# A message-passing kernel on one core: sums on TensorE's column quarters, and a shorter lead of the gathers

## The chip, the core and the metric

The kernel runs on one core of a Trainium2 chip. The core has five engines with a queue of instructions each: TensorE (PE; its weight loads are listed as PEld), VectorE (DVE), ScalarE (ACT), GpSimd (POOL) and SyncE (SP). They meet through semaphores. TensorE writes PSUM (8 banks of 512 floats a partition), ScalarE and VectorE read and write PSUM and the on-chip memory, DMA moves data between that and DRAM. The metric is the device time of one execution in microseconds (us), the median of the runs shown.

## The reference

12500 nodes with 160 features (64 scalars and 32 vectors of three), 400000 edges sorted by their target `dst`. Cut to what matters:

```
h = relu(layernorm(x))
y0, y1 = h0 @ W_l1_0, h1 @ W_l1_1            # per node, times its attribute
w = silu(edge16 @ fc_W1) @ fc_W2             # per edge: w_a 64, w_b 64, w_c 32, w_d 32
mid_a = w_a * y0[src] * e0                   # 64
mid_d = w_d * sum_c(y1[src] * e1)            # 32
mid_b = (w_b * y0[src])[:, :, None] * e1     # 64 x 3
mid_c = (w_c * e0)[:, :, None] * y1[src]     # 32 x 3
z0[dst] += concat(mid_a, mid_d)              # 96
z1[dst] += concat(mid_b, mid_c)              # 96 x 3
out = x + C_S * (h @ W_sc) + C_X * (z @ W_l2) * attribute
```

Per target node 4 x 96 sums are formed over its edges, z0 and the three components of z1, and go through W_l2_0 (96 x 64) and W_l2_1 (96 x 32).

## The kernel before

**Stages.** A node stage computes layernorm and y for all nodes, writes y to DRAM (`y_d`) and leaves x + C_S * (h @ W_sc) in the on-chip tile `acc`. The edge stage, nearly the whole time, adds the messages into `acc`. A last stage that a flag skips here handles edges that fit no window, and stores the result.

**Tiles of the edge stage.** 128 edges are a tile (3125 of them), 4 tiles a batch `b` (782), 3 tiles a window of at most 32 neighbouring target nodes, 4 windows a group `g` (12 tiles, 3 batches, 261 groups).

**What one batch passes through.**
- `load(b)` (L403): every eighth batch SP reads a block of edge features `xe` (L412); for each tile GpSimd issues one indirect DMA (L417), which gathers the 128 source rows of `y_d` into the batch's buffer `yg`. The pool `yg` has 10 buffers (L388), the lead is AHEAD = 8 batches (L554). In this loop GpSimd does nothing but these gathers.
- `hidden_pair` (L434): two matmuls of 32 rows and 512 columns each (L426) and the silu on ScalarE (L431) serve four batches.
- `weigh(b)` (L440): four matmuls of 64 rows (L448) give the edge weights in PSUM `pw` (2 buffers); ScalarE scales them by e0 (L368, four) and copies e1 and the window row beside them (L369).
- `select(b)` (L472): VectorE builds `sel`, for each edge a row of 32 ones and zeros that marks its node in the window (L479, part 3), and the same times each component of e1 (L481, parts 0 to 2).
- `products(b)` (L484): VectorE multiplies weights and gathered rows into `pr`, 256 columns: mid_a 64, mid_d 32, mid_c 3 x 32, w_b * y0 64 (L374 to L381; L381 is the last).
- `sums(b)` (L491): for each tile one product with `sel` (128 edges x 128 columns, four parts of 32) as weights and all 256 columns of `pr` as the moving side (L499). It accumulates over a window's three tiles in a PSUM bank `pz` (2 buffers). Of the 128 x 256 result only the blocks that belong together are used: part 3 with the first 192 columns, parts 0 to 2 with the last 64. After a window ScalarE copies these four blocks to `zs` (L504 once, L506 three times), so that `zs` has a node in each row and 384 columns.
- For the group before: `turn` (three transposes of `zs`, L514, copied by L516), `linear` (three products with `wo`, L523, copied to `os` by L525; VectorE builds `place`, L527), `add` (L535, moves the rows to their places in two node tiles) and `accumulate` (L544, VectorE adds them into `acc`).

fp32 products take two weight loads and two matmuls each in the trace, transposes one: L499 is 3125 products and 6250 matmuls.

**What sets the order.** The order on TensorE, ScalarE and VectorE is written out by hand (L556 to L595): in iteration b come load(b+8), weigh(b+2), one of turn, linear or add of group g-1, select(b+1), products(b+1), at the last batch of a group accumulate(g-1), then sums(b), and hidden_pair in every fourth. Buffers and semaphores do the rest: a gather waits until its `yg` buffer has been read by the products (L381) of the batch that used it ten batches before.

Of the kernel before, what the change touches and what calls it, by code (L numbers as in the profile page):

```python
# [10 lines left out]
F32 = mybir.dt.float32  # L11
I32 = mybir.dt.int32
AF = mybir.ActivationFunctionType
ALU = mybir.AluOpType
# [4 lines left out]
P = 128  # L19
M0 = 64  # L20
M1 = 32
# [4 lines left out]
PC = 256  # L26
ZC = 384
GT = 4
BT = 32
WN = 32  # L30
WT = 3
GW = 4
TG = WT * GW
EG = 8
GN = 8
HN = 2
LO = D - P
EPS = 1e-5
C_S = math.sin(math.pi / 8.0)
# [4 lines left out]
def kernel(  # L44
# [19 lines left out]
    nc = tc.nc  # L64
# [3 lines left out]
    T = n_edges // P  # L68
# [3 lines left out]
    NB = (T + GT - 1) // GT  # L72
# [9 lines left out]
    const = ctx.enter_context(tc.tile_pool(name="const", bufs=1))  # L82
# [5 lines left out]
    ident = const.tile([P, P], F32, name="ident")  # L88
# [90 lines left out]
    w1 = const.tile([P, 2 * FC_H], F32, name="w1")  # L179
    w2 = const.tile([P, NW], F32, name="w2")  # L180

    wo = const.tile([P, 3, D], F32, name="wo")
    wnr = ip.tile([P, 2, 3 * M1], F32, name="wnr")
    wor = ip.tile([P, 3, D], F32, name="wor")
# [16 lines left out]
    def edge_weight_loads():  # L201
        nc.gpsimd.memset(w1, 0.0)
        for i in range(P // FC_IN):
            nc.sync.dma_start(w1[FC_IN * i:FC_IN * (i + 1), FC_H * (i % 2):FC_H * (i % 2 + 1)], fc_w1)
        for i in range(2):
            for to, of, m in ((0, 0, M0), (M0, 2 * M0, M1), (M0 + M1, M0, M0), (2 * M0 + M1, 2 * M0 + M1, M1)):
                nc.sync.dma_start(w2[FC_H * i:FC_H * (i + 1), to:to + m], fc_w2[:, of:of + m])
        nc.gpsimd.memset(wor, 0.0)

        def o1(c):  # L210
            return slice(M0 + M1 * c, M0 + M1 * (c + 1))

        nc.sync.dma_start(wor[0:M0 + M1, 0, 0:M0], w_l2_0)
        for rows, k, c in ((slice(96, P), 0, 0), (slice(0, 32), 1, 1), (slice(32, 64), 1, 2)):
            nc.sync.dma_start(wor[rows, k, o1(c)], w_l2_1[M0:, :])
        for rows, k, c in ((slice(64, P), 1, 0), (slice(0, 64), 2, 1), (slice(64, P), 2, 2)):
            nc.sync.dma_start(wor[rows, k, o1(c)], w_l2_1[0:M0, :])

    def edge_weights():
        nc.vector.tensor_scalar(w2, w2, 1.0 / math.sqrt(FC_H), None, ALU.mult)  # L220
        f = C_X / math.sqrt(10.0 * (M0 + M1))
        nc.vector.tensor_scalar(wo[:, :, 0:M0], wor[:, :, 0:M0], f, None, ALU.mult)
        nc.vector.tensor_scalar(wo[M0:M0 + M1, 0, 0:M0], wo[M0:M0 + M1, 0, 0:M0], 1.0 / math.sqrt(3.0), None, ALU.mult)
        nc.vector.tensor_scalar(wo[:, :, M0:].rearrange("p k (u c) -> p k c u", c=3),
                                wor[:, :, M0:].rearrange("p k (c u) -> p k c u", c=3), f, None, ALU.mult)
# [27 lines left out]
    with (  # L253
# [82 lines left out]
        with tc.manual_schedule(engines=engines):  # L336
# [7 lines left out]
            last = len(steps) - 1  # L344
            for q in range(len(steps) + 4):
                if q <= last and steps[q][2] == 0:
                    g = steps[q][0] + LEAD * GN
# [35 lines left out]
    with (  # L383
# [1 line left out]
        tc.tile_pool(name="prod", bufs=3) as prod,  # L385
        tc.tile_pool(name="ld", bufs=2) as ld,
        tc.tile_pool(name="ev", bufs=2) as evp,
        tc.tile_pool(name="yg", bufs=10) as ygp,  # L388
        tc.tile_pool(name="hid", bufs=4) as hid,
        tc.tile_pool(name="post", bufs=2) as post,  # L390
        tc.tile_pool(name="p_w", bufs=2, space=PSUM) as p_w,
# [3 lines left out]
        blocks, ev4, hids, rows, wts, sels, z_ps, z_sb, zT, o_sb, prs, sums_ps = ({} for _ in range(12))  # L395
# [4 lines left out]
        def windows_of(g):  # L400
            return min(GW, NWIN - g * GW)

        def load(b):  # L403
            blk = b * GT // BT
            if blk not in blocks:

                xe = ld.tile([P, 512], F32, name="xe")
                v = e16[blk * P:(blk + 1) * P, :].rearrange("(s k f) (h c) -> s h f k c", s=4, k=2, h=2)
                for s in range(4):
                    for h in range(2):  # L410
                        lo = 32 * s + FC_IN * h
                        nc.sync.dma_start(xe[lo:lo + FC_IN, :].rearrange("p (k c) -> p k c", k=2), v[s, h])  # L412
                blocks[blk] = xe
            yg = ygp.tile([P, GT, D], F32, name="yg")
            rows[b] = yg
            for k, t in enumerate(tiles_of(b)):
                nc.gpsimd.indirect_dma_start(  # L417
                    out=yg[:, k, :], out_offset=None, in_=y_d,
                    in_offset=bass.IndirectOffsetOnAxis(ap=src_sb[:, t:t + 1], axis=0))
# [69 lines left out]
            prs[b] = pr  # L489

        def sums(b):  # L491
            pr = prs.pop(b)
            for k, t in enumerate(tiles_of(b)):
                g, w = t // TG, t // WT % GW
                if t % WT == 0:
                    z_ps[g, w] = p_z.tile([P, 512], F32, name="pz")
                pz = z_ps[g, w]
                last = t % WT == WT - 1 or t == T - 1
                nc.tensor.matmul(pz[:, 0:PC], sels[g][:, t % TG, :, :], pr[:, k, :], start=t % WT == 0, stop=last)  # L499
                if last:  # L500
                    if w == 0:
                        z_sb[g] = post.tile([P, ZC], F32, name="zs")
                    pz, zs = z_ps.pop((g, w)), z_sb[g][WN * w:WN * (w + 1), :]
                    nc.scalar.activation(zs[:, 0:192], pz[96:P, 0:192], AF.Copy)  # L504
                    for c in range(3):
                        nc.scalar.activation(zs[:, 192 + M0 * c:192 + M0 * (c + 1)],  # L506
                                             pz[WN * c:WN * (c + 1), 192:PC], AF.Copy)

        def turn(g):

            m, zs = WN * windows_of(g), z_sb.pop(g)
            pt = p_x.tile([P, 3, P], F32, name="px")
            for k in range(3):
                nc.tensor.transpose(pt[:, k, :m], zs[:m, P * k:P * (k + 1)], ident[:m, :m])  # L514
            za = post.tile([P, 3, P], F32, name="za")
            nc.scalar.activation(za[:, :, :m], pt[:, :, :m], AF.Copy)  # L516
            zT[g] = za

        def linear(g):
            m, za = WN * windows_of(g), zT.pop(g)  # L520
            po = p_x.tile([P, D], F32, name="px")
            for k in range(3):
                nc.tensor.matmul(po[:m, :], za[:, k, :m], wo[:, k, :], start=k == 0, stop=k == 2)  # L523
            os = post.tile([P, D], F32, name="os")
            nc.scalar.activation(os[:m, :], po[:m, :], AF.Copy)  # L525
            place = post.tile([P, 2, P], F32, name="place")
            nc.vector.tensor_scalar(place.rearrange("p h n -> p (h n)"), iota, at[:, g:g + 1], None, ALU.is_equal)  # L527
            o_sb[g] = os, place
# [23 lines left out]


        AHEAD = 8  # L554
        K = TG // GT
        order = tc.manual_schedule(engines={mybir.EngineType.PE, mybir.EngineType.Activation, mybir.EngineType.DVE})  # L556
        with order:
            for b in range(min(AHEAD, NB)):
                load(b)
            e4_load(0)  # L560
            e4_join(0)
            hidden_pair(0)
            weigh(0)
            if NB > 1:
                weigh(1)
            select(0)
            products(0)
            for b in range(NB):
                g, k = divmod(b, K)
                if b + AHEAD < NB:  # L570
                    load(b + AHEAD)
                q, r = divmod(b, EG * K)
                if r == 0:
                    e4_load(q + 1)
                if r == EG * K - 4:
                    e4_join(q + 1)
                if b + 2 < NB:
                    weigh(b + 2)
                if g:
                    (turn, linear, add)[k](g - 1)  # L580
                if b + 1 < NB:
                    select(b + 1)
                    products(b + 1)
                if g and k == K - 1:
                    accumulate(g - 1)
                    leave_before(g)
                sums(b)
                if b % 4 == 0 and b + 4 < NB:
                    hidden_pair((b + 4) // 2)
            for h in ([NG - 2] if NG > 1 else []) + [NG - 1]:  # L590
                for k, stage in enumerate((turn, linear, add, accumulate)):
                    if h == NG - 1 or min(k, K - 1) > (NB - 1) % K:
                        stage(h)
                        if k == 3:
                            leave_before(h + 1)  # L595
# [4 lines left out]
    with (  # L600
# [10 lines left out]
        n = nc.values_load(far_i[0:1, 0:1], min_val=0, max_val=1)  # L611
        with tc.For_i(0, n, 1) as _:
            with tc.For_i(0, ZR, P) as r:
                nc.sync.dma_start(z_d[ds(r, P), :], zero)
            with tc.For_i(0, TP // GT, 1) as g:
# [15 lines left out]
                yg = fp.tile([P, GT, D], F32, name="f_yg")  # L631
# [9 lines left out]
                for k in range(GT):  # L641
                    nc.tensor.matmul(pw[:, k, 0:NW], hT[:, P * k:P * (k + 1)], w2[0:FC_H, :],
                                     start=True, stop=True)
                tmp = fp.tile([P, GT, 4, M1], F32, name="f_tmp")
                scale(pw, ev, GT)
                pr = fp.tile([P, GT, PC], F32, name="f_pr")
                multiply(pr, tmp, pw, yg, GT)
                for k in range(GT):
                    pd = fpp.tile([P, P], F32, name="f_pd")
                    nc.tensor.transpose(pd, df[:, k:k + 1].to_broadcast([P, P]), ident)  # L650
                    sel = fp.tile([P, P], F32, name="f_sel")
# [82 lines left out]
```

## Time and profile before

| | us |
|---|---|
| three runs | 5686.64, 5694.77, 5710.15 |
| median | 5694.77 |
| profiled execution | 5716.56 |
| its span | 5714.8 |
| mean granted TensorE clock | 0.776 |

Busy time in the profiled execution: PE 3840.1 us, DVE 2902.1, ACT 2645.1, POOL 3024.8. The matmuls of L499 are busy for 1930.1 us (462 ns each, 6250 of them), the copies of L504 and L506 for 337.8 and 669.8 us, the gathers of L417 for 2983.4 us (955 ns each).

How to read the page: a group's line gives line, engine, operation, what it writes and reads, its count, then after the first bar busy time and mean ns of one, after the second the idle time of the engine just before these instructions and what ended most of it. The chain is followed back from the last instruction; its shares are of the span. A row of the timeline gives start, length, engine, line, operation, count, and in brackets the idle time before and its releaser. "remote" (in the chain: another core or an unknown queue) is what is written where no releaser was found in the semaphore records; "issue" is time in which an engine waited for nothing that the profile shows.

### The profile page before, as it was taken

Reading aid. Unit: us, or ns where it says so; the run is one execution under the profiler, and the core shown is the slowest. Engines: PE = TensorE matmul, PEld = TensorE weight load, DVE = VectorE, ACT = ScalarE, POOL = GpSimd, SP = SyncE. Lnnn points to the kernel's source line nnn. Section 1 sums busy time; section 2 is a strip of 40 time slices with the busy share of each in tenths; the row PEclk is TensorE's granted clock in tenths of the full one; section 3 lists DMA queues with packets and bytes.
Section 4 is the critical chain, followed back from the end, with each engine's and each line's share of the span. In section 5 each row is a group of like instructions: output and inputs, shape, how many; then the busy total and the mean of one; then the engine's idle time right before and its main releaser. Section 6 shows DMA issues by size and latency. Waiting matters only on the chain.

```text
span 5714.8 us, 61466 instructions
## 1 busy us (share of the span) xinstructions
PE 3840.1 (67%) x17265; PEld 2679.8 (47%) x17265; DVE 2902.1 (51%) x7407; ACT 2645.1 (46%) x9217; POOL 3024.8 (53%) x3150
## 2 busy tenths in 40 slices
PE   6476676666666666666667667666667766666766
PEld 5344444444444444444444445444444444444544
DVE  7454455444455455454555445544445554545555
ACT  5244444444444444444444444444444444444445
POOL 3655555555555555555555555555555555555553
PEclk9677777787777777777777777777777778788778
DMA  4211111211111111111112112111111121232211
GB/s 140 62 53 52 53 54 49 54 52 52 52 51 54 52 53 52 52 53 50 54 53 55 51 53 55 52 52 52 51 52 52 54 54 53 54 88 55 55 49 54
DMA packets 233168, 319.85 MB, mean 56 GB/s; under 512 B 65754, under 2 KB 182566, under 8 KB 232566
## 3 DMA queue, kind: packets, MB, share of 16 engines
q0 software_dynamic: 150000, 256.20, 16.7%
q1 hardware_dynamic: 69026, 51.24, 3.1%
q10 hardware_dynamic: 13796, 8.44, 0.5%
q8 instruction: 139, 2.28, 0.2%
q14 instruction: 207, 1.70, 0.1%
HBM read 299.62 MB, written 16.00 MB: 55 GB/s over the span
## 4 chain that ended last, share of the span: by engine, by line
PE 52%; another core or an unknown queue 23%; ACT 13%; issue 8%; DVE 3%; DMA 0%; SPq 0%; DVEq 0%; ACTq 0%
PE pz L499 25%; PE pw L448 10%; PE px L426 6%; ACT pw L368 5%; PE px L514 4%; PE px L523 4%; ACT zs L506 3%; PE px L535 3%; ACT zs L504 2%; ACT pw L369 1%; ACT hT L431 0%; DVE h L283 0%; DVE tmp L376 0%; DVE tmp L374 0%
## 5 line engine op out<-in xcount | busy, mean ns | idle before, releaser
L417 POOL DMA_INDIRECT yg<-y_d,src_sb x3125 | 2983.4, 955 | 2542.2 <-DVE pr L381 1641.0
L499 PE MATMUL pz<-pr,sel 128*128 128x256 f32 x6250 | 1930.1, 462 | 151.1 <-ACT zs L506 114.2
L368 ACT ACTIVATE pw<-pw,ev 128x96 f32<-128x96 f32 x3125 | 985.3, 315 | 1679.1 <-remote 1048.8
L499 PEld LDWEIGHTS pz<-pr,sel 128*128 128x128 f32 x6250 | 1443.4, 242 | 406.4 <-ACT zs L506 132.4
L544 DVE SCALAR_TENSOR_TENSOR acc<-px,a_sb,acc 128x160 f32 x522 | 200.2, 384 | 1765.5 <-remote 1292.0
L514 PE MATMUL px<-ident,zs 128*128 128x128 f32 (+1 forms) x783 | 268.9, 428 | 876.2 <-ACT zs L504 804.3
L448 PE MATMUL pw<-w,hT 64*128 64x192 f32 x6250 | 839.2, 394 | 12.9 <-DVE pr L381 8.1
L448 PEld LDWEIGHTS pw<-w,hT 64*128 64x128 f32 x6250 | 579.6, 216 | 469.4 <-issue 269.8
L426 PE MATMUL px<-xe,w 32*128 32x512 f32 x782 | 415.6, 789 | 526.1 <-remote 422.1
L479 DVE TENSOR_TENSOR sel<-iota,pw 128x128 f32<-128x128 f32 x782 | 223.5, 286 | 951.5 <-ACT pw L369 591.7
L504 ACT ACTIVATE zs<-pz 32x192 f32<-32x192 f32 x1042 | 337.8, 324 | 776.2 <-PE pz L499 312.9
L506 ACT ACTIVATE zs<-pz 32x64 f32<-32x64 f32 x3126 | 669.8, 214 | 41.8
L514 PEld LDWEIGHTS px<-ident,zs 128*128 128x128 f32 (+1 forms) x783 | 130.3, 181 | 1025.9 <-ACT zs L504 857.1
L376 DVE TENSOR_REDUCE tmp<-tmp 128x128 f32<-128x384 f32 x782 | 463.5, 593 | 26.8
L481 DVE TENSOR_TENSOR sel<-sel,pw 128x384 f32<-128x384 f32 x782 | 432.5, 553 | 26.7
L379 DVE TENSOR_TENSOR pr<-pw,yg 128x384 f32<-128x384 f32 x782 | 427.9, 547 | 0.0
L374 DVE TENSOR_TENSOR tmp<-yg,pw 128x384 f32<-128x384 f32 x782 | 427.8, 547 | 0.0
L426 PEld LDWEIGHTS px<-xe,w 32*128 32x128 f32 x782 | 107.8, 227 | 678.2 <-remote 470.9
L535 PE MATMUL px<-os,place 128*128 128x160 f32 x1044 | 236.7, 354 | 207.0 <-issue 175.0
L431 ACT ACTIVATE hT<-px 128x512 f32<-128x512 f32 x391 | 221.6, 596 | 300.5 <-remote 194.0
L377 DVE TENSOR_TENSOR pr<-pw,yg 128x256 f32<-128x256 f32 x782 | 323.6, 414 | 0.0
L378 DVE TENSOR_TENSOR pr<-pw,yg 128x256 f32<-128x256 f32 x782 | 323.4, 414 | 0.0
(83 smaller groups left out, 1902.3 us busy)
## 6 DMA issues: line engine op xcount, KB each, us to landing
yg<-y_d,src_sb POOLq DMA_INDIRECT x3125
xe<-in_e SPq DMA_DIRECT2D x784, 32.0 KB
xt<-in_x SPq DMA_DIRECT2D x12, 640.0 KB
y_d<-ys ACTq DMA_DIRECT2D x12, 640.0 KB
out<-acc SPq DMA_DIRECT2D x11, 640.0 KB
raw<-in_e SPq DMA_DIRECT2D x32, 192.0 KB
dst_i<-in_dst SPq DMA_DIRECT2D x1, 1568.0 KB
src_sb<-in_src SPq DMA_DIRECT2D x1, 1568.0 KB
```

Source lines behind the costliest of these rows:

```text
L368: nc.scalar.activation(pw[:, k, 0:96], pw[:, k, 0:96], AF.Copy, scale=ev[:, k, 0:1])
L374: nc.vector.tensor_tensor(tmp[:, :n, 0:3, :], y1, wt[:, :n, NW:NW + 3].unsqueeze(3).to_broadcast([P, n, 3, M1]), ALU.mult)
L376: nc.vector.tensor_reduce(tmp[:, :n, 3, :], tmp[:, :n, 0:3, :].rearrange("p t c u -> p t u c"), AX.X, ALU.add)
L379: nc.vector.tensor_mul(pr[:, :n, 96:192].rearrange("p t (c u) -> p t c u", c=3), wt[:, :n, M0:96].unsqueeze(2).to_broadcast([P, n, 3, M1]) ...
L417: nc.gpsimd.indirect_dma_start(out=yg[:, k, :], out_offset=None, in_=y_d, in_offset=bass.IndirectOffsetOnAxis(ap=src_sb[:, t:t + 1], axis=0))
L426: nc.tensor.matmul(ph, w1[r, :], xe[r, :], start=True, stop=True)
L448: nc.tensor.matmul(pw[:, k, 0:NW], hT[r, o:o + P], w2[r, :], start=True, stop=True)
L481: nc.vector.tensor_tensor(sel[:, :, 0:3, :], sel[:, :, 3:4, :].to_broadcast([P, n, 3, WN]), wt[:, :n, NW:NW + 3].unsqueeze(3).to_broadcast ...
L499: nc.tensor.matmul(pz[:, 0:PC], sels[g][:, t % TG, :, :], pr[:, k, :], start=t % WT == 0, stop=last)
L504: nc.scalar.activation(zs[:, 0:192], pz[96:P, 0:192], AF.Copy)
L506: nc.scalar.activation(zs[:, 192 + M0 * c:192 + M0 * (c + 1)], pz[WN * c:WN * (c + 1), 192:PC], AF.Copy)
L514: nc.tensor.transpose(pt[:, k, :m], zs[:m, P * k:P * (k + 1)], ident[:m, :m])
```

## The change

**Sums.** `sums` makes seven products for a tile instead of one. The weights are one part of `sel` each, 32 columns wide, and the result goes to 32 of the 128 PSUM partitions, a column quarter of TensorE: parts 0, 1, 2 with w_b * y0 (64 columns) to quarters 0, 1, 2; part 3 with mid_a and mid_d (96 columns) to quarter 3; part 3 again with one component of mid_c (32 columns) to each of quarters 0, 1, 2. A window takes 96 columns of the bank, and all four windows of a group lie side by side in one bank, which is copied once per group, 384 columns of all 128 partitions.

**After the sums.** The quarters now are the four kinds of sums (z1 by component, z0) and the columns the 96 features, so `turn` makes four transposes, one for each window, `linear` four products of 96 rows, one for each kind, against the plain weights `wz` (64 columns for z0, 32 for each component), and `os` is copied in two pieces, the second of which puts the components side by side. `wz` costs two more DMAs and two scalings in the setup; `wo` stays for the last stage.

**Gathers.** `load` is split: `features` keeps the lead of 8 batches, the gathers get RUN = 2 and a pool of 3 buffers instead of 10.

```
+SC = M0 + M1
...
+        nc.sync.dma_start(wz[:, 0:M0], w_l2_0)
+        nc.sync.dma_start(wz[:, M0:], w_l2_1)
...
+        nc.vector.tensor_scalar(wz, wz, f, None, ALU.mult)
+        nc.vector.tensor_scalar(wz[M0:, 0:M0], wz[M0:, 0:M0], 1.0 / math.sqrt(3.0), None, ALU.mult)
...
-        tc.tile_pool(name="yg", bufs=10) as ygp,
+        tc.tile_pool(name="yg", bufs=3) as ygp,
...
-        def load(b):
+        def features(b):
...
+        def load(b):
             yg = ygp.tile([P, GT, D], F32, name="yg")
...
         def sums(b):
             pr = prs.pop(b)
             for k, t in enumerate(tiles_of(b)):
                 g, w = t // TG, t // WT % GW
-                if t % WT == 0:
-                    z_ps[g, w] = p_z.tile([P, 512], F32, name="pz")
-                pz = z_ps[g, w]
-                last = t % WT == WT - 1 or t == T - 1
-                nc.tensor.matmul(pz[:, 0:PC], sels[g][:, t % TG, :, :], pr[:, k, :], start=t % WT == 0, stop=last)
-                if last:
-                    if w == 0:
-                        z_sb[g] = post.tile([P, ZC], F32, name="zs")
-                    pz, zs = z_ps.pop((g, w)), z_sb[g][WN * w:WN * (w + 1), :]
-                    nc.scalar.activation(zs[:, 0:192], pz[96:P, 0:192], AF.Copy)
-                    for c in range(3):
-                        nc.scalar.activation(zs[:, 192 + M0 * c:192 + M0 * (c + 1)],
-                                             pz[WN * c:WN * (c + 1), 192:PC], AF.Copy)
+                if t % TG == 0:
+                    z_ps[g] = p_z.tile([P, 512], F32, name="pz")
+                sel = sels[g][:, t % TG, :, :]
+                first, last = t % WT == 0, t % WT == WT - 1 or t == T - 1
+                for r, part, c, lo, n in [(s, s, 192, 0, M0) for s in range(3)] + [(3, 3, 0, 0, SC)] + \
+                        [(s, 3, SC + M1 * s, M0, M1) for s in range(3)]:
+                    o = SC * w + lo
+                    nc.tensor.matmul(z_ps[g][WN * r:WN * (r + 1), o:o + n], sel[:, part, :], pr[:, k, c:c + n],
+                                     start=first and lo == 0, stop=last and (lo > 0 or r == 3))
+                if t % TG == TG - 1 or t == T - 1:
+                    zs = post.tile([P, GW, SC], F32, name="zs")
+                    n = windows_of(g)
+                    nc.scalar.activation(zs[:, :n, :].rearrange("p w c -> p (w c)"), z_ps.pop(g)[:, 0:SC * n], AF.Copy)
+                    z_sb[g] = zs
...
         def turn(g):
-            for k in range(3):
-                nc.tensor.transpose(pt[:, k, :m], zs[:m, P * k:P * (k + 1)], ident[:m, :m])
-            za = post.tile([P, 3, P], F32, name="za")
-            nc.scalar.activation(za[:, :, :m], pt[:, :, :m], AF.Copy)
+            for w in range(n):
+                nc.tensor.transpose(pt[0:SC, w, :], zs[:, w, :], ident)
+            za = post.tile([SC, 4, GW, WN], F32, name="za")
+            nc.scalar.activation(za.rearrange("p s w n -> p w s n")[:, :n, :, :],
+                                 pt[0:SC, :n, :].rearrange("p w (s n) -> p w s n", n=WN), AF.Copy)
...
         def linear(g):
-            for k in range(3):
-                nc.tensor.matmul(po[:m, :], za[:, k, :m], wo[:, k, :], start=k == 0, stop=k == 2)
+            for r, lo, wd, o in [(3, 0, M0, 0)] + [(s, M0, M1, M0 + M1 * s) for s in range(3)]:
+                nc.tensor.matmul(po[:m, o:o + wd], za[:, r, :n, :], wz[:, lo:lo + wd], start=True, stop=True)
             os = post.tile([P, D], F32, name="os")
-            nc.scalar.activation(os[:m, :], po[:m, :], AF.Copy)
+            nc.scalar.activation(os[:m, 0:M0], po[:m, 0:M0], AF.Copy)
+            nc.scalar.activation(os[:m, M0:].rearrange("p (u c) -> p c u", c=3),
+                                 po[:m, M0:].rearrange("p (c u) -> p c u", c=3), AF.Copy)
...
         AHEAD = 8
+        RUN = 2
...
             for b in range(min(AHEAD, NB)):
+                features(b)
+            for b in range(min(RUN, NB)):
                 load(b)
...
                 if b + AHEAD < NB:
-                    load(b + AHEAD)
+                    features(b + AHEAD)
+                if b + RUN < NB:
+                    load(b + RUN)
```

More of the change, by code (lines that the diff above doesn't have):

```diff
@@ L180 @@
     w2 = const.tile([P, NW], F32, name="w2")
+    wz = const.tile([M0 + M1, M0 + M1], F32, name="wz")
     wo = const.tile([P, 3, D], F32, name="wo")
@@ L509, in turn @@
-        def turn(g):
-            m, zs = WN * windows_of(g), z_sb.pop(g)
-            pt = p_x.tile([P, 3, P], F32, name="px")
-            for k in range(3):
-                nc.tensor.transpose(pt[:, k, :m], zs[:m, P * k:P * (k + 1)], ident[:m, :m])
-            za = post.tile([P, 3, P], F32, name="za")
-            nc.scalar.activation(za[:, :, :m], pt[:, :, :m], AF.Copy)
+                if t % TG == 0:
+                    z_ps[g] = p_z.tile([P, 512], F32, name="pz")
+                sel = sels[g][:, t % TG, :, :]
@@ new lines, in sums @@
+                if t % TG == TG - 1 or t == T - 1:
[3 more added lines that the diff above has]
+                    z_sb[g] = zs
+        def turn(g):
+            n, zs = windows_of(g), z_sb.pop(g)
+            pt = p_x.tile([P, GW, P], F32, name="px")
+            for w in range(n):
[3 more added lines that the diff above has]
+                                 pt[0:SC, :n, :].rearrange("p w (s n) -> p w s n", n=WN), AF.Copy)
@@ L517, in turn @@
             zT[g] = za
         def linear(g):
-            m, za = WN * windows_of(g), zT.pop(g)
+            m, n, za = WN * windows_of(g), windows_of(g), zT.pop(g)
             po = p_x.tile([P, D], F32, name="px")
-            for k in range(3):
-                nc.tensor.matmul(po[:m, :], za[:, k, :m], wo[:, k, :], start=k == 0, stop=k == 2)
+            for r, lo, wd, o in [(3, 0, M0, 0)] + [(s, M0, M1, M0 + M1 * s) for s in range(3)]:
+                nc.tensor.matmul(po[:m, o:o + wd], za[:, r, :n, :], wz[:, lo:lo + wd], start=True, stop=True)
```

## Prediction

> **What bounds the kernel now.** I read the page first: busy shares, chain, costliest groups.
>
> ```profile
> span 5714.8 us, 61466 instructions
> PE 3840.1 (67%) x17265; PEld 2679.8 (47%) x17265; DVE 2902.1 (51%) x7407; ACT 2645.1 (46%) x9217; POOL 3024.8 (53%) x3150
> PE 52%; another core or an unknown queue 23%; ACT 13%; issue 8%; DVE 3%; DMA 0%; SPq 0%; DVEq 0%; ACTq 0%
> L417 POOL DMA_INDIRECT yg<-y_d,src_sb x3125 | 2983.4, 955 | 2542.2 <-DVE pr L381 1641.0
> L499 PE MATMUL pz<-pr,sel 128*128 128x256 f32 x6250 | 1930.1, 462 | 151.1 <-ACT zs L506 114.2
> L448 PE MATMUL pw<-w,hT 64*128 64x192 f32 x6250 | 839.2, 394 | 12.9 <-DVE pr L381 8.1
> L504 ACT ACTIVATE zs<-pz 32x192 f32<-32x192 f32 x1042 | 337.8, 324 | 776.2 <-PE pz L499 312.9
> L506 ACT ACTIVATE zs<-pz 32x64 f32<-32x64 f32 x3126 | 669.8, 214 | 41.8
> ```
>
> The reader is to see that no engine is full, and that 23% of the chain hangs on a releaser which this one-core program should not have. The table of waits says who meets it, the scaling of the weights (L368) and the accumulation (L544), both of which wait for TensorE:
>
> ```profile
> POOL yg L417 <- DVE pr L381: 1641.0, 282, 10.3
> DVE acc L544 <- remote: 1292.0, 166, 9.7
> ACT pw L368 <- remote: 1048.8, 161, 18.7
> ```
>
> The timeline around one such wait:
>
> ```profile
> 3016.54 0.92 PE L448 MATMUL pw<-w,hT 64*128 64x192 f32 x8
> ...
> 3024.34 0.95 POOL L417 DMA_INDIRECT yg<-y_d,src_sb  x1 [0.30 <-issue]
> 3027.44 1.36 ACT L368 ACTIVATE pw<-pw,ev 128x96 f32<-128x96 f32 x4 [7.40 <-remote]
> ...
> 3032.41 0.95 POOL L417 DMA_INDIRECT yg<-y_d,src_sb  x1 [7.12 <-DVE pr L381]
> ```
>
> L448 ended at 3017.46, but ScalarE, which waits for nothing else, could read its result only at 3027.44, 2.2 us after GpSimd's last gather ended (3025.29). Over the whole trace: batches whose L448 ends in the first 5 us of an unbroken run of gathers are seen by ScalarE within a median of 0.04 to 0.24 us; those that end 6 to 9 us into a run, after 8 to 9 us, and nearly always 2.2 us after the run's end. I call this a **hold**: late in a long run of gathers TensorE's completions do not arrive. The trace shows that it happens, not why.
>
> So the loop is a cycle. 196 of the 324 runs have 12 gathers, three batches, 14.8 us (a gather takes 0.95, the next begins 0.30 later). Then GpSimd is idle for 7.2 us: 2.2 until the hold ends, 5.0 for scaling (1.6), selection and products (3.3), whose end frees a buffer. That is 22.0 us for three batches, 7.3 each; over the loop (5714.8 less about 165 before the first sums, 782 batches) it is 7.1. Outside a hold the batches follow each other at 3.3 to 3.8 us.
>
> **The change, part by part.**
>
> *Sums, per edge tile.* Out: one product of 128x256, two matmuls in the trace; unhindered, L499 issues one each 216 ns, 0.84 ns a column, 1.73 us a batch, and 427 ns (3.4 us) at the halved clock that follows each idle stretch (mean granted 0.776). In: seven products, 14 matmuls and 14 weight loads, 56 of each a batch. Widths 64, 64, 64, 96, 32, 32, 32 add up to 384 columns instead of 256. The trace has no matmul on a column quarter, so I bound it. *Below:* the quarters stream side by side, as the two 64-row halves of L448 do (pairs start 6 or 7 ns apart, one pair each 162 ns): 96 columns twice, 160 ns a tile, 0.64 us a batch. *Above:* every load-and-matmul pair costs the 109 ns of the shortest sustained pairs in the trace (L302, L303, L317, 128 columns wide): 56 x 0.109 = 6.1 us. *Taken:* one quarter after another with the loads hidden, as L499 hides its 128-column loads: 384 x 2 x 0.84 = 645 ns, 2.6 us a batch, 0.9 more than now. L499 is nearest, since it has the same 128 rows of contraction and the same loads beside matmuls.
>
> The Trainium skill, "TensorEngine Tiling (Array Packing)", section Performance Considerations, speaks against this change: it gives each matmul an overhead of about 60 cycles, and warns against tiling a dimension that is already small, as 32 and 64 columns are. "TensorE: Matmul & The Clock Gate", section Back-to-back issue gap, gives N=128 about 81 ns a matmul with its load; by that, an estimate, the sums would take 56 x 0.081 = 4.5 us. For it, section Packing small matmuls of that page gives three column tiles 2.38 times the speed. No run here shows any of this yet.
>
> *Evacuation, per group of three batches.* Out: four L504 (0.324) and twelve L506 (0.214), 3.86 us. In: one copy of 384 columns (0.49, as L516) and a second copy in os (about 0.25). ScalarE saves 3.1 us a group, 1.0 a batch, 820 us in all, nearly all beside other work, since ScalarE is busy 46% of the time. Its worth lies between a hold's end and the next one: there eight copies (1530.21 to 1532.26) stand before the next scaling, and L514, then L499, wait behind the last of them. They go, so the next L448 (1535.77 in that cycle) can follow the freeing of its PSUM buffer at 1533.5: some 2 us earlier.
>
> *Turn, linear, add.* Three transposes become four (+0.11 a group), six linear matmuls of 160 columns become eight of 64 or 32 (six at 0.136 against eight at 0.03 to 0.11: -0.6 to +0.05). Two more loads and two scalings in the setup: under 1 us, beside relate.
>
> *Gathers.* The same 3125; nothing is moved past them on POOL's queue, which holds only gathers here. Up to 10 batches ahead become 2, 3 buffers for 10. A gathered batch needs 5.0 us and lands about 1.35 later; it is asked for when products(b-1) end and needed two batches later, 7.4 us or more: hidden, and costs what is missing when batches come faster than 5.0. The first run shrinks from 48 gathers, in which holds of 14 us lie, to 12: gain 0 to 40. At the end only 3 batches, not 10, run without gathers: 7 x (7.1 - 3.7) = 24 lost. I count both at nothing together. In the cycle the buffers hardly matter: GpSimd now stops after the three freed buffers, and will again.
>
> **The sum.** In a cycle the fourth L448 ends about 1.7 us after the holds begin (run start 1533.58 plus 5 is 1538.6; L448 ended at 1540.28, seen at 1549.14). The missing copies bring it 2 us forward, the longer sums push it back by up to 0.9; in cold stretches the sums cost 3.4 now. So it is won about every second time. Four batches need a run of 20 and the same 7.2: 27.2 us. Two such cycles, one of each kind, carry 7 batches in 49.2 us: 7.03, against 22.0/3 = 7.33 now: -4.2% of the loop's 5550 us, -230. Profiled: 5717 - 230 = 5487. The profiled execution took 5716.56, 22 above the median of 5694.77; against the median, 5465. **Forecast: 5465.**
>
> **Rivals.**
>
> *Gathers broken into single batches.* With three buffers and slower sums, GpSimd may have to wait after every batch, and a hold ends early in each gap. The trace has such a stretch: from 5319.94 to 5342.92 runs of four gathers with gaps of 1.0 us, four batches in 22.98, 5.75 each. All along: 782 x 5.75 + 165 = 4660, 4640 against the median. For it: buffers are the only thing that stops GpSimd. Against: after each hold three batches are ready, and at 3.7 us a batch they free buffers faster than the 5.0 of a gathered batch.
>
> *Slower: TensorE becomes the bound by its instruction count.* At 109 ns a pair the sums take 6.1 us; the rest of TensorE's batch is 0.65 (L448), about 0.6 for the switches around it (0.33 idle before L448), 0.6 (a third of turn, linear and add) and 0.27 (L426): 8.2 in all. 782 x 8.2 + 165 = 6580. It decides as soon as the sums exceed 7.1 - 2.1 = 5.0 us, 89 ns a pair. For it: TensorE's instructions rise from some 44 a batch to 145, and it leads the chain with 52%. Against: L448's eight pairs take 0.65 us, 81 ns a pair, side by side.
>
> *The cycle stays at three batches.* Copies and sums were hidden anyway: the time stays at 22 us for three, 5680 to 5710; or the lost tail and holds that come earlier make it 5730 to 5900.
>
> **How the numbers follow.** Forecast (5300 to 5660) 0.33; single batches (4500 to 5300) 0.24; TensorE bound (5900 to 7000) 0.29; cycle unchanged, 0.14, half of it within 0.5%, half slower. What differs by under 0.5% this kernel's times cannot tell from no change. Faster 0.57, same 0.07, slower 0.36. As both signs hold much, the forecast's own range is 5300 to 5660; the range for 8 in 10 goes from 4650 to 6600, the ends of the two rivals.
>
> **What will show it.** Right: zs copies at some 130 us in all, runs of 12 and 16 gathers with 7.2 us between them, idle time of L375 (the old L368) still put down to "remote". Single batches: runs of four, idle before L426 (the gathers) ended by DVE in most batches, a higher clock. TensorE bound: gathers and scaling idle behind it, its matmuls unbroken, few "remote". It would be wrong altogether if the hold depends on how many instructions TensorE completes, not on the gathers: then 3.3 times the instructions would hold far longer.

## The result, and the profile after

The changed kernel takes 6394.39 us, the median of four runs (6359.61 to 6441.03); the kernel before took 5690.87 beside it (four runs). The ratio is 1.121, 95% interval 1.116 to 1.126: slower by 12%, where 5465 us was forecast. The profiled execution of the changed kernel took 6359.61 us.

These lines of its page answer to those shown of before; L426 is the old L417, L388 the old L381, L457 the old L448, L514 the old L499, L375 the old L368; L519 stands for L504 and L506.

```profile
span 6357.8 us, 134649 instructions
PE 4344.4 (68%) x55546; PEld 2966.7 (47%) x55546; DVE 2886.3 (45%) x7409; ACT 1796.8 (28%) x5571; POOL 3021.3 (48%) x3150
PE 57%; issue 24%; another core or an unknown queue 11%; ACT 4%; DVE 2%; DMA 0%; POOL 0%; DVEq 0%; ACTq 0%
L426 POOL DMA_INDIRECT yg<-y_d,src_sb x3125 | 2979.9, 954 | 3217.2 <-DVE pr L388 2367.9
L514 PE MATMUL pz<-pr,sel 128*32 128x64 f32 (+2 forms) x43750 | 1661.2, 262 | 1379.3 <-issue 1360.1
L514 PEld LDWEIGHTS pz<-pr,sel 128*32 128x32 f32 x43750 | 1172.3, 140 | 1908.0 <-issue 1888.4
L519 ACT ACTIVATE zs<-pz 128x384 f32<-128x384 f32 (+1 forms) x261 | 127.2, 487 | 739.1 <-remote 391.6
```

ScalarE lost 848 us of work, and GpSimd's gathers take what they took (2979.9 us), yet GpSimd sits idle 675 us longer before them (3217.2 against 2542.2). A new word leads the waits: "issue" before the matmuls and loads of the sums, time in which TensorE waited for nothing that the profile shows. It was 8% of the chain and is 24%. The table of waits (engine, line, what it waited for, us, times, longest):

```profile
POOL yg L426 <- DVE pr L388: 2367.9, 424, 20.5
PEld pz L514 <- issue: 1888.4, 2786, 2.0
ACT pw L375 <- PE pw L457: 1399.1, 514, 15.3
...
ACT pw L375 <- remote: 1001.7, 107, 14.4
```

The timeline shows what an "issue" wait is. A run of eight gathers began at 3004.06; its last four, and TensorE beside them:

```profile
3009.13 0.95 POOL L426 DMA_INDIRECT yg<-y_d,src_sb  x1 [0.30 <-issue]
...
3010.46 0.22 PE L514 MATMUL pz<-pr,sel 128*32 128x64 f32 x1 [0.19 <-issue]
...
3011.17 0.43 PE L514 MATMUL pz<-pr,sel 128*32 128x64 f32 x4 [0.49 <-issue]
...
3012.59 0.35 PE L514 MATMUL pz<-pr,sel 128*32 128x96 f32 x5 [0.99 <-issue]
...
3012.90 0.95 POOL L426 DMA_INDIRECT yg<-y_d,src_sb  x1 [0.30 <-issue]
...
3014.02 0.34 PE L514 MATMUL pz<-pr,sel 128*32 128x32 f32 x3 [1.08 <-issue]
...
3015.44 1.22 PE L514 MATMUL pz<-pr,sel 128*32 128x64 f32 x41 [1.08 <-issue]
...
3015.53 1.36 ACT L375 ACTIVATE pw<-pw,ev 128x96 f32<-128x96 f32 x4 [10.43 <-remote]
...
3019.54 1.51 PE L514 MATMUL pz<-pr,sel 128*32 128x64 f32 x56
```

From 3010.46 TensorE gets off one to five matmuls at a time, at steps of 0.71 us or twice that. The last gather ends at 3013.85; 1.6 us later the remaining 41 go in 1.22 us. The next batch, in a pause of the gathers, sends all 56 in 1.51 us, 27 ns each. So the hold of the prediction here delays the starts of TensorE's instructions themselves, not only the news of their completions.

Averaged over the runs of 12 gathers with a break of over 2.5 us behind them (191 before, 92 after), before's TensorE starts 80 instructions (loads and matmuls) in the first 8 us of a run and then 3.2 a us until 16 us. After's starts 106 in the first 5 us and then 3.4 a us. By 16.5 us 107 and 144 have started: 2.4 batches of 44 before, but just one batch of 142 after. It is not one fixed number that gets through: in the same way 82 have started in the kernel called pairs below and 133 in halves.

Summed over the whole trace (gathers under 0.6 us apart make one run): GpSimd's runs take 3,843 us before and 3,802 after, the breaks between them 1,681 and 2,394 us. The breaks grow by 713 us, the span by 643: the breaks hold the whole loss. In runs TensorE starts 12.6 instructions a us in the changed kernel, in breaks 25.7.

The mean granted TensorE clock also fell, from 0.776 to 0.639. That is no sufficient cause: in runs below it is 0.549 where 0.9% is lost, and 0.75 where 0.5% is.

### The profile page after: what moved, and what is told of

The parts are those of the page before. It is cut to its first block, busy times and chain, and to the rows that moved or that the text cites. A ratio compares the mean times of both kernels' runs of the same rounds, so it can differ in the third digit from the quotient of the medians.

```text
span 6357.8 us, 134649 instructions
## 1 busy us (share of the span) xinstructions
PE 4344.4 (68%) x55546; PEld 2966.7 (47%) x55546; DVE 2886.3 (45%) x7409; ACT 1796.8 (28%) x5571; POOL 3021.3 (48%) x3150
## 4 chain that ended last, share of the span: by engine, by line
PE 57%; issue 24%; another core or an unknown queue 11%; ACT 4%; DVE 2%; DMA 0%; POOL 0%; DVEq 0%; ACTq 0%
PE pz L514 21%; PE pw L457 17%; PE px L435 6%; PE px L537 5%; PE px L551 4%; PE px L527 3%; ACT pw L375 2%; ACT hT L440 1%; DVE tmp L381 0%; ACT zs L519 0%; DVE tmp L383 0%; DVE pr L386 0%; ACT pw L376 0%; DVE acc L560 0%
## 5 line engine op out<-in xcount | busy, mean ns | idle before, releaser
L426 POOL DMA_INDIRECT yg<-y_d,src_sb x3125 | 2979.9, 954 | 3217.2 <-DVE pr L388 2367.9
L514 PE MATMUL pz<-pr,sel 128*32 128x64 f32 (+2 forms) x43750 | 1661.2, 262 | 1379.3 <-issue 1360.1
L514 PEld LDWEIGHTS pz<-pr,sel 128*32 128x32 f32 x43750 | 1172.3, 140 | 1908.0 <-issue 1888.4
L375 ACT ACTIVATE pw<-pw,ev 128x96 f32<-128x96 f32 x3125 | 985.4, 315 | 2732.7 <-PE pw L457 1399.1
L457 PE MATMUL pw<-w,hT 64*128 64x192 f32 x6250 | 1272.4, 496 | 166.5 <-issue 128.7
L457 PEld LDWEIGHTS pw<-w,hT 64*128 64x128 f32 x6250 | 830.7, 275 | 572.9 <-issue 436.3
L381 DVE TENSOR_TENSOR tmp<-yg,pw 128x384 f32<-128x384 f32 x782 | 427.8, 547 | 0.0
L537 PE MATMUL px<-wz,za 96*128 96x32 f32 (+1 forms) x2088 | 366.6, 323 | 43.5 <-issue 22.0
L551 PE MATMUL px<-os,place 128*128 128x160 f32 x1044 | 360.7, 494 | 49.8 <-ACT hT L440 38.5
L537 PEld LDWEIGHTS px<-wz,za 96*128 96x128 f32 x2088 | 333.7, 240 | 123.6 <-issue 83.2
L519 ACT ACTIVATE zs<-pz 128x384 f32<-128x384 f32 (+1 forms) x261 | 127.2, 487 | 739.1 <-remote 391.6
L551 PEld LDWEIGHTS px<-os,place 128*128 128x128 f32 x1044 | 258.7, 308 | 164.4 <-issue 93.8
L527 PE MATMUL px<-ident,zs 128*96 128x128 f32 x1042 | 247.4, 382 | 122.0 <-ACT zs L519 118.1
```

Source lines behind the costliest of these rows:

```text
L375: nc.scalar.activation(pw[:, k, 0:96], pw[:, k, 0:96], AF.Copy, scale=ev[:, k, 0:1])
L381: nc.vector.tensor_tensor(tmp[:, :n, 0:3, :], y1, wt[:, :n, NW:NW + 3].unsqueeze(3).to_broadcast([P, n, 3, M1]), ALU.mult)
L426: nc.gpsimd.indirect_dma_start(out=yg[:, k, :], out_offset=None, in_=y_d, in_offset=bass.IndirectOffsetOnAxis(ap=src_sb[:, t:t + 1], axis=0))
L457: nc.tensor.matmul(pw[:, k, 0:NW], hT[r, o:o + P], w2[r, :], start=True, stop=True)
L514: nc.tensor.matmul(z_ps[g][WN * r:WN * (r + 1), o:o + n], sel[:, part, :], pr[:, k, c:c + n], start=first and lo == 0, stop=last and (lo > ...
L527: nc.tensor.transpose(pt[0:SC, w, :], zs[:, w, :], ident)
```

## The experiments

*First theory:* while indirect gathers run, TensorE can complete only so many instructions, so the change costs by its 76,562 more (111,092 records against 34,530). *Rivals:* the quarter products are slow in themselves; or the short lead leaves the products without rows.

**Each half of the change alone.** *Gathers alone* is before with

```
-        tc.tile_pool(name="yg", bufs=10) as ygp,
+        tc.tile_pool(name="yg", bufs=3) as ygp,
...
+                if b + RUN < NB:
+                    load(b + RUN)
```

and `RUN = 2`. 

> The kernel before with one part of the change alone: rows gathered two batches ahead, three row buffers; the sums stay four products of 256 columns a batch. First theory (while gathers run, TensorE's instructions complete at a limited rate, so the time follows their number, which stays 34,530 records here): within 2% of before, 5,580 to 5,800 us. Rival (the short lead leaves the products without rows, and that is the loss): 6,000 us or more.

Measured 5711.45 us, 0.997 of before (0.993 to 1.001). *Sums alone* is after with `RUN = 8` and ten row buffers. 

> The kernel after with the old gathers: eight batches ahead and ten row buffers; the sums stay 28 quarter products a batch. First theory (the number of TensorE's instructions against the gathers' run): still slow, about 6,390 us or more, since longer runs of gathers give longer holds. Rival (the short lead): back at about 5,700 us.

Measured 6388.31 us, 1.121 of before (1.112 to 1.129). The sums carry the whole loss, the lead none of it.

**The number of instructions, on the kernel before.** *Halves* issues the same sums in twice as many products:

```
-                nc.tensor.matmul(pz[:, 0:PC], sels[g][:, t % TG, :, :], pr[:, k, :], start=t % WT == 0, stop=last)
+                for c in range(0, PC, P):
+                    nc.tensor.matmul(pz[:, c:c + P], sels[g][:, t % TG, :, :], pr[:, k, c:c + P],
+                                     start=t % WT == 0 and c == 0, stop=last and c > 0)
```

> The kernel before with each tile's sums issued as two products of 128 columns: the same columns and results, 8 more instructions a batch (a load and a matmul for each of four tiles: 44 become about 52 by loads and matmuls). First theory (a limit on the number of instructions): slower, by a share of the 700 us that about 100 more instructions a batch cost in the kernel after, 55 to 150 us. Rival (only what the array computes counts, or only the gathers): within 0.5% of before.

Measured 5938.41 us, 1.041 (1.034 to 1.047), more than expected; each product is two passes, so the records rise by 16 a batch and not by 8 (47,030 in all). What the halves would cost without gathers was not measured. The new "issue" wait appears here too:

```profile
L500 PE MATMUL pz<-pr,sel 128*128 128x128 f32 x12500 | 2057.5, 327 | 740.6 <-issue 401.6
```

*Pairs* goes the other way: two weight products of 384 columns for four of 192. Not shown are the weights `wd`, in which zeros fill the halves that must not mix, and the edge features' loads, which become twice as many.

```
-            for k in (0, 2, 1, 3):
-                if k < n:
-                    r = slice(FC_H * (k // 2), FC_H * (k // 2 + 1))
-                    o = P * (b % 2 * 2 + k % 2)
-                    nc.tensor.matmul(pw[:, k, 0:NW], hT[r, o:o + P], w2[r, :], start=True, stop=True)
+            for k in range(0, n, 2):
+                o, m = P * (b % 2 * 2 + k // 2), min(2, n - k)
+                nc.tensor.matmul(pw[:, k:k + m, 0:NW], hT[:, o:o + P], wd[:, 0:m, :], start=True, stop=True)
```

> The kernel before with the four weight products of a batch (192 columns from 64 rows each) joined to two of 384 columns from 128 rows, against block-diagonal weights: the same results, two instruction pairs fewer a batch. First theory (a limit on the number of instructions): faster, by 25 to 150 us. Rival (number doesn't count, columns and rows do): within 0.5% of before or up to 1% slower, since no product runs beside its neighbour on the other half of the rows any more.

Measured 5624.80 us, 0.985 (0.980 to 0.991): faster than both kernels, although TensorE's busy time rises from 3840.1 to 4014.4 us.

**No gathers.** Both kernels with one batch's rows gathered once:

```
+            if "yg" not in still:
+                still["yg"] = ygp.tile([P, GT, D], F32, name="yg")
+                for k in range(GT):
+                    nc.gpsimd.indirect_dma_start(
...
+            rows[b] = still["yg"]
```

> The kernel before with the rows of the first batch gathered once and used by all 782 batches: the other 3,121 gathers are left out, so that the sums are of other rows than the reference's. First theory (only while gathers run do TensorE's instructions complete slowly): the chain goes at the pace of the busiest engine, VectorE's 2,900 us and ScalarE's 2,645 us, so 3,000 to 3,500 us. Rival (a batch's pace is TensorE's own, whatever GpSimd does): above 4,000 us.

> The kernel after with the same edit (one batch's rows gathered once, the other 3,121 gathers left out, other sums than the reference's). First theory: the 76,562 records more on TensorE cost nothing without gathers (56 quarter matmuls took 1.51 us unhindered), so within 100 us of the kernel before without gathers, or below it. Rival (the quarter products are slow in themselves): 500 us or more above it.

Measured 3070.57 and 3111.31 us (one run each), beside 5843.91 for the kernel before on that chip. First the page of before without gathers, then of after without gathers:

```profile
PE 2960.8 (96%) x17265; PEld 2193.1 (71%) x17265; DVE 2850.5 (93%) x7407; ACT 2614.0 (85%) x9217; POOL 45.7 (1%) x29
```

```profile
PE 2611.1 (84%) x55546; PEld 1960.4 (63%) x55546; DVE 2837.3 (91%) x7409; ACT 1805.2 (58%) x5571; POOL 45.4 (1%) x29
```

Without gathers the 76,562 instructions more even make TensorE less busy, by 350 us. The first rival falls; what costs is these instructions beside gathers.

**What in a gather does it.** The kernel before with each tile's rows loaded directly, first on SyncE's queue, then on GpSimd's:

```
-                nc.gpsimd.indirect_dma_start(
-                    out=yg[:, k, :], out_offset=None, in_=y_d,
-                    in_offset=bass.IndirectOffsetOnAxis(ap=src_sb[:, t:t + 1], axis=0))
+                r = t * 37 % (N // P) * P
+                nc.sync.dma_start(yg[:, k, :], y_d[r:r + P, :])
```

> The kernel before with each tile's 128 rows loaded by one direct DMA of 128 neighbouring rows, on SyncE's queue: the same bytes into the same buffers, no gather by GpSimd, other rows than the reference's. If it is GpSimd's indirect gathers that hold TensorE back: 3,000 to 3,600 us, as without any gathers. If it is the rows' traffic itself: about 5,700 us.

> As e7_rows_by_sp (128 neighbouring rows a tile in the gathers' place, other rows than the reference's), but each load is issued on GpSimd's queue, which writes its descriptors in software, where SyncE's are made by hardware. If it is GpSimd's writing of descriptors that slows TensorE's instructions: well above e7_rows_by_sp's 3,074 us, 4,000 to 5,700 us. If only the indirect gather does it: 3,050 to 3,300 us.

> As e9_rows_by_pool (128 neighbouring rows a tile by a direct load on GpSimd's queue, other rows than the reference's). On a chip with the hold (before at 5,690 us or more): 4,000 to 5,700 us if GpSimd's writing of descriptors holds TensorE back, 3,050 to 3,300 us if only the indirect gather does. On a chip without it (before at 4,071 us): 3,071 us, and then nothing is told.

By SyncE 3074.25 us (before: 5843.91 on that chip). By GpSimd 3071.38 and, in a repetition, 3072.69 us, but both on chips on which the kernel before takes 4,071 us, of which below; the third run met a chip where before took 5778.22: 3072.07 us. So neither the 256 MB (150,000 packets on the queue in both) nor these loads issued by GpSimd hold TensorE back, and the indirect gathers do. Whether it is their instruction, their scattered rows or the length of their runs is not separated: the direct loads take neighbouring rows, and they come mostly in fours of 2.13 us with breaks between, while the hold shows 5 us or more into a run. Long unbroken runs of direct loads beside the sums were not tried.

**Half the passes.** After with `sel` and `pr` declared as bf16, so that the factors of the sums are rounded. 

> The kernel after with the selections and the products written as bf16 (the sums are then of rounded factors): the 28 quarter products of a batch stand, but each should be one pass of a load and a matmul and no longer two, so 111,092 records become about 67,300. First theory (their number): half of the excess over before goes at least, 5,950 to 6,150 us. Rival (the quarters' order, banks or waits, not their number): 6,300 us or more.

Measured 5900.32 us beside 5843.91: 1.009 (1.004 to 1.014). Most of the excess is gone with 43,750 of the records, but more than a plain count explains. Per record added or taken away against before, from the medians: halves 223 us / 12,500 = 18 ns, pairs 90 / 6,248 = 14 ns, the change 704 / 76,562 = 9 ns, and here 56 / 32,812 = 1.7 ns. The number gives the direction in each, but not the size; that a small or bf16 instruction costs less than a large f32 one would fit these four and is not shown, since the last two also save ScalarE's copies. What exactly is limited stays open.

**A chip without the hold.** Pairs with bf16 sums, and with bf16 weight products as well (the factors rounded). 

> The kernel with the paired weight products (v1_pairs), and the selections and products written as bf16, so that the four products of a batch's sums are one pass each: 28,282 records on TensorE become about 15,800 to 22,000. First theory (the number of TensorE's instructions while gathers run): faster again, by about 14 ns (before to v1_pairs: 85 us over 6,248 records) for each record taken away, 90 to 170 us below v1_pairs, so 0.955 to 0.97 of before. Rival (what is left is the gathers' own pace and the rate of VectorE): within 0.5% of v1_pairs.

> As v2_pairs_bf16, and the weight products of bf16 factors too (the hidden layer and its weights rounded): about 3,100 records fewer once more. First theory: 30 to 60 us below v2_pairs_bf16. Rival: within 0.5% of it.

Measured 4093.04 and 4092.57 us, but beside 4071.47 for the kernel *before*: this chip runs it in 28% less time than any so far. So both kernels were run again unchanged. 

> The kernel after, unchanged, beside the kernel before. On a chip where TensorE's instructions are held back during gathers (before at 5,690 us or more) 1.11 to 1.13 of before, as measured. On a chip where they are not (before at 4,071 us): by the first theory the 76,562 records more cost nothing, and the gathers' own pace of about 1.25 us sets the time, 0.99 to 1.01 of before. By the rivals (quarter products slow in themselves, or the lead too short) 1.03 or more there too.

> The kernel before, unchanged, for a trace on this chip. Where it takes 4,071 us, by the first theory its gathers follow each other with no breaks and TensorE issues at its full rate in the middle of them; where it takes 5,690 us or more, runs of 12 gathers and breaks of 7 us as known.

> As e9_rows_by_pool (128 neighbouring rows a tile by a direct load on GpSimd's queue, other rows than the reference's). On a chip with the hold: 4,000 to 5,700 us if GpSimd's writing of descriptors holds TensorE back, 3,050 to 3,300 us if only the indirect gather does. On a chip without it: 3,071 us as before.

> The paired weight products and bf16 sums again. On a chip with the hold, by the first theory 0.955 to 0.97 of before. On a chip without it 1.005 of before, as measured.

They met another chip of this kind. After: 4091.98 us against 4071.60, 1.005 (1.003 to 1.007). Pairs with bf16: 4093.49, 1.005 (1.004 to 1.007). After's page and timeline there:

```profile
span 4091.4 us, 134649 instructions
DVE 23%; POOL 22%; DMA 22%; issue 20%; PE 6%; DVEq 1%; ACT 1%; POOLq 0%; ACTq 0%
L426 POOL DMA_INDIRECT yg<-y_d,src_sb x3125 | 2960.2, 947 | 972.4 <-issue 745.2
L514 PE MATMUL pz<-pr,sel 128*32 128x64 f32 (+2 forms) x43750 | 932.3, 250 | 0.0
```

```profile
3000.02 0.95 POOL L426 DMA_INDIRECT yg<-y_d,src_sb  x1 [0.30 <-issue]
...
3005.02 0.95 POOL L426 DMA_INDIRECT yg<-y_d,src_sb  x1 [0.30 <-issue]
...
3005.67 1.51 PE L514 MATMUL pz<-pr,sel 128*32 128x64 f32 x56
...
3006.27 0.95 POOL L426 DMA_INDIRECT yg<-y_d,src_sb  x1 [0.30 <-issue]
```

From the thirteenth to the last the gathers follow each other every 1.25 us, and in the midst of them all 56 matmuls go in 1.51 us; L514's matmuls have no idle time before them. From 1500 to 2500 us TensorE starts 28.0 instructions a us (8.6 in before's trace there) and nothing holds it. The gathers alone set the time: 3125 at 1.25 us are 3,910 us, and some 160 lie around them. Before's gathers there have no gap over 0.6 us; after's have one, of 20.03 us, behind the 12th gather, where the short lead first runs out of buffers. That is its 20 us. Pairs with bf16 has no such gap; there the first gather starts late (166.69 us for 138.45 in before).

The 1.51 us are a figure of the halved clock. Two batches of the same trace, then the same two stretches, in which the third number from the end is the granted clock:

```profile
2004.03 0.90 PE L514 MATMUL pz<-pr,sel 128*32 128x64 f32 x56
2010.35 1.51 PE L514 MATMUL pz<-pr,sel 128*32 128x64 f32 x56
...
2004.03:2004.93 0.90, 0.90 (x57) 0.79 (x56) 0.02 (x1) 0.83 (x3) 0.59 (x2) 1.00 0.31 91
2010.35:2011.86 1.51, 1.51 (x57) 1.37 (x56) 0.47 (x1) 0.42 (x2) 1.21 (x2) 0.50 0.34 88
```

So 56 matmuls with their loads take 0.90 us at the full clock, 16 ns each, and 27 ns each at half of it.

Two last runs of pairs with bf16 were to tell its gain on a chip with the hold. 

> The paired weight products and bf16 sums once more. On a chip with the hold (before at 5,690 us or more): by the first theory 0.955 to 0.97 of before, by the rival 0.98 to 0.99 as v1_pairs. On a chip without it 1.005 of before, as measured.

> The paired weight products and bf16 sums, a last time. On a chip with the hold (before at 5,690 us or more): by the first theory 0.955 to 0.97 of before, by the rival 0.98 to 0.99 as v1_pairs. On a chip without it 1.005 of before, as measured.

Both met chips without it, one of them the chip of the runs just shown: 4092.81 (1.005; 1.004 to 1.007) and 4091.90 (1.005; 1.003 to 1.007). So its gain where the hold exists was not measured.

The runs with all their gathers, except those of pairs with bf16; breaks are GpSimd's over the whole trace, as worked out above:

| kernel | TensorE records | granted clock | breaks, us | ratio to before |
|---|---|---|---|---|
| pairs | 28,282 | 0.809 | 1,603 | 0.985 |
| before | 34,530 | 0.776 | 1,681 | 1 |
| gathers alone | 34,530 | 0.777 | 1,709 | 0.997 |
| halves | 47,030 | 0.761 | 1,887 | 1.041 |
| after with bf16 sums | 67,342 | 0.549 | 1,902 | 1.009 (chip with before at 5,844) |
| after | 111,092 | 0.639 | 2,394 | 1.121 |
| sums alone | 111,092 | 0.642 | 2,403 | 1.121 |
| before, no hold | 34,530 | 0.938 | 0 | 1 |
| after, no hold | 111,092 | 0.750 | 20 | 1.005 |

## Why the prediction was wrong

**What bounds the kernel** was read rightly: TensorE's work is held back in runs of gathers, GpSimd then finds no free buffer, and the time is gathers plus breaks.

**The step that failed** is in the sum: "Four batches need a run of 20 and the same 7.2". It took the hold for something that the gathers' run alone sets, and let the 7.2 us of idle time stand with 3.3 times the instructions. It does not stand. After a run of 12 the break is 9.4 us where before's trace has 6.6 on average, after a run of 8 it is 6.2 for 4.6. And no run grew to 16: the 442 runs have 4 (194), 8 (155) or 12 (92) gathers and one has 5, 1.8 batches a run for 2.4 (782 batches in 324 runs). Because the runs are shorter, the mean over all breaks hardly moves (5.4 us for 5.2); there are 441 of them for 323. The prediction's last sentence names this very case, but no chance was given to it. The prediction's own timeline had a hint: L448 had run to its end 10 us before ScalarE could read its result, so it was completions that were late. That an engine with three times as many to complete might be later still was worth a chance; the hint alone did not show it.

**The sums' size**, taken at 2.6 us between 0.64 and 6.1, is 0.90 us unhindered at the full clock, where L499's 0.84 ns a column was also read (1.51 us at half). The quarters stream nearly side by side, close to the lower bound; unhindered the new sums even take less than the old 1.73 us. The number that was too high pointed towards slower, and still the forecast was faster, so this size is not the cause. The 4.5 us estimated from the 81 ns that the Trainium skill gives for N=128 in "TensorE: Matmul & The Clock Gate", section Back-to-back issue gap, are five times the 0.90 measured here with 32 columns of weights and 32 to 96 moving ones.

**The evacuation** was right in size (ScalarE 848 us less, 820 worked out; copies of zs 127 us, 130 expected) and no run shows a gain from it. The step "brings it 2 us forward" rested on a next product that would complete once it was issued; in after, L375 still waits 1001.7 us for "remote" and 1399.1 more for L457. Nor does the saving pay where there is no hold, since the gathers set the time there.

**The gathers' lead** was rightly counted at nothing: 0.997 alone. Both of its terms came too: in the trace of gathers alone the products of the twelfth batch end at 252.0 us for 277.0 before, and the last nine batches' products take 53.0 us for 32.7. On chips without the hold it costs the 20 us at the start.

**The rival "TensorE becomes the bound by its instruction count"**, 6580 us, lies near the measured time, for a wrong reason. Its price of 109 ns a pair is seven times the 16 measured at the full clock and four times the 27 at half, its condition (sums over 5.0 us) isn't met, and its signs are absent: L514's matmuls are broken up and "remote" remains. That the number of instructions counts was right; that it counts by TensorE's own time was not: 3111 us without gathers and 4092 beside unbroken ones show that TensorE can work off the same instructions in half and in two thirds of the time.

**Single batches at a faster pace** didn't come about: runs of four are common (194), but the breaks behind them average 3.0 us where that rival had gaps of 1.0.

The 1.121 is therefore a statement about chips that show the hold; on the others the same change costs 0.5%.

## What to carry to other kernels

When the profile shows an engine's completions arriving late for no reason that it can name, count how many instructions of that engine an edit adds or removes: fewer, larger matmuls were worth 1.5% here, and the same sums cut in halves cost 4%. Take what paces the loop (here the gathers) and sum its unbroken runs and its breaks; a loss that lies wholly in the breaks is a wait, whatever the busy shares say. And before a stall is taken for a property of the kernel, run the unchanged kernel on a second chip.

## What the runs showed of the hardware

- The same program took 5,691, 5,715, 5,844 and 5,778 us on some occasions (at least three chips) and 4,071 to 4,072 (medians) on four others (three other chips). On the first kind TensorE falls to a few instructions a us late in runs of indirect gathers (3.4 a us in after's runs of 12); on the second it doesn't (28.0 a us). What sets the two apart, the chip or something else that ran on it, is open, and so is whether the recording of the trace, which all these executions share, has a part in it.
- Indirect gathers of 128 rows by GpSimd take 0.95 us and start every 1.25 us; a direct load of 128 neighbouring rows on the same queue took 0.54 us and held nothing back even on a chip with the hold, in runs of mostly four.
- 56 matmuls of 32 to 96 columns on four column quarters, with 56 loads, took 0.90 us at a granted clock of 1.0 and 1.51 us at 0.5.
